# A graph layer on one core: one pipeline stage per iteration, more gathers put together from columns

## The chip, the cores and the metric

The kernel runs on one core of a Trainium2 chip. The metric is the device time of one execution in microseconds, as the median of several runs. The core has five engines that work side by side, each through its own queue in order: TensorE (PE, with weight loads shown as PEld), VectorE (DVE), ScalarE (ACT), GpSimd (POOL) and SyncE (SP), which starts DMAs.

## The reference

12500 nodes with 64 features, 200000 edges sorted by target (`dst`), with random sources (`src`):

```python
ssp(v) = softplus(v) - log(2)
gates = (ssp(edge_attr @ We1 + be1) @ We2 + be2) * (1 - sigmoid(5 * (dist - 3.5)))
h = ssp(concat(x[src], x[dst]) @ Wn1 + bn1) @ Wn2 + bn2
message_sum = zeros_like(x).at[dst].add(h * gates)
new = x + (ssp(message_sum @ Ws1 + bs1) @ Ws2 + bs2)
out = layernorm(x + new)
```

Edge layers go from 64 to 64 features, node layers from 128 to 128 and to 64. All is float32.

## The kernel before

The edges are cut into 391 groups of 512. A group is four lots (K = 4) of 128 edges, and one lot's source rows come by one indirect DMA that POOL issues (`gather`, L204): 128 rows of 64 floats into the tile `xg`. The half of the first node layer that belongs to the targets is a table in DRAM (x times the lower half of Wn1, plus bias), written in 98 chunks of 128 nodes in the first iterations (`chunk`, `keep_chunk`). Since targets are sorted, 256 edges touch a window of at most W = 42 nodes: SP loads the window of the table (`load`, L224, tile `wns`), and a one-hot matrix beside the source rows (`onehot`, L277) picks the row for each edge.

One group runs through these steps, named as in the code:

- PE: `transposes` of the four lots with their one-hot parts into PSUM `tx` (L283). ACT: `xcopy` to SBUF (L291).
- PE: layer 1 into PSUM tile `z`: bias (L296), edge half (L301), node half (L308). The tile `z` is two banks, with two buffers; 768 columns hold layer 1, then come 84 columns for scatter sums and 128 spare ones.
- ACT: `exps` (L322) and `logs` (L325) into SBUF tile `u`. DVE: `softplus` (L330), one operation on `u` and on `z`.
- PE: layer 2 into PSUM `gh` (bias L347, edge L354, node L359). DVE: `hcut` (L368) and `message` (L372).
- PE: `scatter` (L376), the messages times the one-hot matrices, into the 84 columns of a later `z`. DVE: `window` (L396), two additions into `sums` at addresses held in registers.

Some lots are not gathered. x also lies in SBUF as columns (`xh`), and for a chosen lot 128 copies of one column each, at addresses from registers (`columns`, L259, on ACT and DVE), build the source rows already transposed. `read_columns` (L242) loads those addresses from SBUF into registers, `choose` (L271) picks the right half, and an extra product with `wn1_twice` takes the place of the gather. `COLUMNS = (8, 16)` is the number of columns per iteration on DVE and on ACT, and `slots_by_columns` plans from it which lots they are: 70 of them, so 71 groups have three gathers (one of them because of the padding at the end) and 320 have four.

`busy` (L334) is a product that nobody reads, issued so that PE doesn't pause: one before the node half of layer 1 where no chunk stands there, one before layer 2. Whenever the sums of a block of 512 nodes are complete, a node block follows (25 of them): `hidden` (L415), `clamp` (L430, L431), `logs`, `ssp`, second layer (L446), `add`, and the layer norm (`square`, `variance`, `root`, `scale` L472, `store`), spread over later iterations by `BLOCK_STEPS`.

The order on every engine is written by hand (`manual_schedule`): what stands earlier in the loop body is earlier in that engine's queue, and the tile framework adds waits where data or buffers need them. Iteration i gathers group i + 3, does layer 1 for group i + 1, layer 2 and messages for group i and the scatter for group i - 2. A gather waits for its buffer, one of eight: in iteration i for the scatter of group i - 5, which PE issues three iterations earlier. The last groups and the last node block are written out by hand after the loop, and from twelve groups before the end (`CLOSE`) two scatters move one iteration closer.

Of the kernel before, what the change touches and what calls it, by code (L numbers as in the profile page):

```python
# [92 lines left out]
def chunk_of(i, NCH):  # L93

    c = i + CHUNKS
    return c if i >= 0 and c < NCH else None


def nodes_ready(g, NCH):

    return min(NCH, CHUNKS * (1 + max(0, (g - LOADS) // CHUNKS))) * P


@with_exitstack
def gnn_resnorm_kernel(ctx: ExitStack, tc: tile.TileContext, a: dict, out: bass.AP, E: int):
# [10 lines left out]
    REST = LOADS + 2  # L116
# [9 lines left out]
    loads = inner.enter_context(tc.tile_pool(name="loads", bufs=LOADS + 2, side="right"))  # L126
# [44 lines left out]
    columns_at = const.tile([P, sum(columns_of)], I32, name="columns_at")  # L171
    wn1_twice = const.tile([P, 2 * D], F32, name="wn1_twice")
# [22 lines left out]
    def gather(g, part=range(K), needs=()):  # L195

        if part[0] == 0:
            xgs[g] = loads.tile([P, K, P], F32, name="xg", bufs=AHEAD + BEHIND)
        xg = xgs[g]
        for k in part:  # L200
            if padding(g, k) or (g, k) in by_columns:
                nc.vector.memset(xg[:, k, :D], 0.0)
                continue
            behind(note(("gather", g), nc.gpsimd.indirect_dma_start(  # L204
                out=xg[:, k, :D], out_offset=None, in_=x,
                in_offset=bass.IndirectOffsetOnAxis(ap=src_i[:, g, k : k + 1], axis=0))), *needs)
            needs = ()
# [3 lines left out]
    def load(g):  # L211
        old = ("scatter", g - LOADS - 4)
# [18 lines left out]
    column_at, columns_done, whole = [[], []], [0, 0], []  # L231
# [4 lines left out]
    def read_columns(i, queue):  # L236

        if columns_left(i, queue) <= 0:
            return
        n, count = columns_done[queue], COLUMNS[queue]  # L240
        p, q = (n // count) % P, queue * columns_of[0] + n // (count * P) * count
        column_at[queue] = nc.values_load_multi_w_load_instructions(  # L242
            columns_at[p : p + 1, q : q + count], engines=[engines[queue][1]], min_val=xh_at,
            max_val=xh_at + 4 * (half_n - 1), skip_runtime_bounds_check_because="src holds rows of x")[1]
# [19 lines left out]
    def choose(pool):  # L264

        while whole:
            queue, g, k = slot = whole.pop(0)
# [6 lines left out]
    xTs, zs, us, ss, ghs, hs, msgs, scs = ({} for _ in range(8))  # L274
# [4 lines left out]

    def transposes(g, *needs):  # L280
        tx = tx_tile()[:DW].rearrange("f (k e) -> f k e", k=K)
# [7 lines left out]
    def xcopy(g):  # L289
        xT = work.tile([DW, K, P], F32, name="xT", bufs=3)  # L290
# [3 lines left out]
    def layer1_bias(g, *needs):  # L294
        zs[g] = z_tile()
# [21 lines left out]
    every, edge, node = slice(0, 3 * HE), slice(0, HE), slice(HE, 3 * HE)  # L317

    def exps(g, part=every):
        if part.start == 0:  # L320
            us[g] = work.tile([P, 3 * HE], F32, name="u")
        nc.scalar.activation(us[g][:, part], z_of(g)[:, part], AF.Exp)  # L322

    def logs(g, part=every):
        nc.scalar.activation(us[g][:, part], us[g][:, part], AF.Ln, bias=one)  # L325

    def softplus(g, part=every):
        if part.start == 0:
            ss[g] = work.tile([P, 3, 2, P], F32, name="s", bufs=3)
        nc.vector.scalar_tensor_tensor(ss[g].rearrange("p i t e -> p (i t e)")[:, part], us[g][:, part], BIG,  # L330
                                       z_of(g)[:, part], OP.min, OP.max)
# [7 lines left out]
    opened = {}  # L339

    def busy_before_layer2(g):
        opened[g + 1] = gh_tile()
        busy(opened[g + 1][:, :P])

    def layer2_bias(g):
        gh = opened.pop(g) if g in opened else gh_tile()
# [9 lines left out]
    def layer2_node(g):  # L356
        for h in range(2):
            for t in range(2):
                nc.tensor.matmul(ghs[g][:, 1, 2 * t + h, :], ss[g][:, 1 + h, t, :], wn2, start=False,  # L359
                                 stop=h == 1 and t == 1, skip_group_check=True)  # L360

# [4 lines left out]
    def hcut(g):  # L366
        hs[g] = work.tile([P, K, D], F32, name="h")
        nc.vector.tensor_mul(hs[g], ghs[g][:, 1], cut[:, g, :].to_broadcast([P, K, D]))  # L368

    def message(g):  # L370
        msgs[g] = work.tile([P, K, D], F32, name="msg", bufs=3)
# [26 lines left out]
    def node_block(first, n, pool):  # L398
# [7 lines left out]
        def tile3(name):  # L406
            return pool.tile([P, 2, 2, D], F32, name=name, bufs=3)[:p, :nq]
# [4 lines left out]
        def hidden(z):  # L412
            t["z"] = z[:, :HE]
            for q in range(nq):
                nc.tensor.matmul(t["z"], ws1[:, q].rearrange("f o d -> f (o d)"),  # L415
                                 sums[:, first + q * HE : first + (q + 1) * HE], start=q == 0, stop=q == nq - 1,
                                 skip_group_check=True)

        def fetch():
            t["y"] = tile3("y")  # L420
            nc.sync.dma_start(t["y"], x[rows, :].rearrange("(q p k) d -> p q k d", q=nq, k=2))
# [5 lines left out]

        def clamp():
            t["l"], t["zb"] = (pool.tile([P, HE], F32, name=name, bufs=2) for name in ("l_s", "zb"))
            nc.vector.tensor_scalar(t["l"], t["z"], packed["bs1"], BIG, OP.add, OP.min)  # L430
            nc.vector.tensor_scalar(t["zb"], t["z"], packed["bs1"], None, OP.add)  # L431
# [8 lines left out]
        def layer2(z):  # L440
            slots = t["l"].rearrange("f (p k) -> f k p", k=2)
            t["u"] = z[:p, :HE].rearrange("p (q k d) -> p q k d", q=2, k=2)
            nc.tensor.matmul(z[:p, :HE], ones3[:, :p], rs3.rearrange("q k d -> q (k d)"), start=True,
                             stop=False, skip_group_check=True)
            for k in range(2):
                nc.tensor.matmul(t["u"][:, :, k, :], slots[:, k, :p], ws2, start=False, stop=k == 1,  # L446
                                 skip_group_check=True)

        def add():
            nc.vector.scalar_tensor_tensor(t["y"], t["y"], 2.0, t["u"][:, :nq], OP.mult, OP.add)  # L450

        def square():
            t["y2"] = tile3("y2")
# [23 lines left out]
        return [Part(None, fetch), Part(hidden, clamp), Part(None, logs), Part(None, center), Part(None, ssp),  # L477
                Part(layer2, add), Part(None, square), Part(None, variance), Part(None, root), Part(None, scale),
                Part(None, store)]

    def node_part(part):
        if part.tensor:
            part.tensor(gh_tile())
        part.others()

    with tc.manual_schedule():
# [4 lines left out]
        xT = sums[: D + 1, : NCH * P].rearrange("d (c p) -> d c p", p=P)  # L491
# [3 lines left out]
        def load_x(first, last):  # L495
            nc.sync.dma_start(xT[:, first:last, :], a["xT"][:, first:last, :])

        dst_h = prep.tile([P, NR, HE], I32, name="dst_h")
# [5 lines left out]
        nc.sync.dma_start(src_i[:, :HEAD, :], cols[:, :HEAD, :])  # L504
        nc.scalar.dma_start(dst_h, a["dst_h"])
        load_x(0, CHUNKS)
        nc.scalar.dma_start(consts[:, :FIRST], a["consts"][:, :FIRST])
        nc.sync.dma_start(dst_i[:, :HEAD, :], targets[:, :HEAD, :])
# [5 lines left out]
        load_x(CHUNKS, 2 * CHUNKS)  # L514

        for g in range(AHEAD):
            gather(g)
# [24 lines left out]
        for c in range(CHUNKS):  # L542
            nc.tensor.matmul(ps[:, c, :], xT[:, c, :], wnb, start=True, stop=True)
# [4 lines left out]
        spread = prep.tile([P, NR, P], F32, name="spread")  # L548
        base_b = prep.tile([P, NR * P], F32, name="base_b")
# [66 lines left out]

        def highest():
# [10 lines left out]
        def far():  # L628
            ps = tx_tile()
# [13 lines left out]
        def chunk(c, z):  # L643
            if c % CHUNKS == 0:
                tbs[c // CHUNKS] = piece()
            nc.tensor.matmul(z, xT[:, c, :], wnb, start=True, stop=True, skip_group_check=True)
# [6 lines left out]
        cuts = [2 * CHUNKS, 4 * CHUNKS, 6 * CHUNKS, 9 * CHUNKS, 12 * CHUNKS, NCH]  # L653
        beside = {0: [lambda: nc.sync.dma_start(src_i[:, HEAD:, :], cols[:, HEAD:, :])],
                  1: [lambda: nc.sync.dma_start(columns_i, a["columns"]), load_wn1, lambda: load_xh(0)],
                  2: [lambda: load_xh(1), far], 3: [lambda: load_xh(2)], 4: [lambda: load_xh(3), places],
                  5: [lambda: load_x(cuts[0], cuts[1])],
                  6: [lambda: nc.sync.dma_start(dst_i[:, HEAD:, :], targets[:, HEAD:, :])],
                  7: [lambda: load_x(cuts[1], cuts[2])], 10: [lambda: load_x(cuts[2], cuts[3])],
# [292 lines left out]
```

## Time and profile before

| | |
|---|---|
| median of three runs | 2363.53 us (2359.99 to 2370.90) |
| profiled execution | 2389.88 us, span 2388.1 us, mean granted clock 0.981 |
| PE | 1970.5 us busy (83% of the span), 12897 instructions |
| PE weight loads | 1656.7 us (69%) |
| ACT | 1511.2 us (63%), 7412 instructions |
| POOL | 1417.0 us (59%), 1497 instructions, 1493 of them gathers |
| DVE | 1293.9 us (54%), 5966 instructions |

Busy times of an engine are added over its instructions; an engine that waits is not busy. All figures of the trace are of the profiled execution. A row of the timeline gives the start, the duration, the engine, the source line, the operation with its output and inputs, and in brackets the idle time before it with what ended it. A row of the groups gives the count, the total busy time and the mean in nanoseconds of one, then the idle time just before.

### The profile page before, as it was taken

The page shows a single profiled execution, that of the slowest core. Times are in us where ns is not written, and L with a number is a line of the kernel's source. Part 1 is how long each engine was busy: PE and PEld are TensorE (multiplying, and loading weights), DVE is VectorE, ACT ScalarE, POOL GpSimd, SP SyncE. Part 2 cuts the span into 40 slices and gives each one's busy share as a digit, 9 for nine tenths or more (in the row PEclk, how much of TensorE's full clock was granted, in tenths as well). Part 3 has the DMA queues.
Part 4 walks back from the last instruction along what each step waited for, and adds up shares of the span by engine and source line. Part 5 has one row for each costly group of instructions (what it writes and reads, how often), then busy time and mean ns, then how long its engine had stood idle before and what let it go on. Part 6 is the DMA issues. An engine that isn't in the chain of part 4 may idle for free.

```text
span 2388.1 us, 48209 instructions
## 1 busy us (share of the span) xinstructions
PE 1970.5 (83%) x12897; PEld 1656.7 (69%) x12897; DVE 1293.9 (54%) x5966; ACT 1511.2 (63%) x7412; POOL 1417.0 (59%) x1497
## 2 busy tenths in 40 slices
PE   6788888888888888888888888888888888888877
PEld 4666677767776776677677667766777767777765
DVE  4355555555555555555555555555555555555544
ACT  3466666666666666666666666666666666666653
POOL 5665665666666666666666666665665666666650
PEclk9799999999999999999999999999999999999988
DMA  6332232322222222222222222222222222222220
GB/s 185 85 91 68 56 75 56 77 61 71 54 57 56 53 59 54 57 56 62 53 59 55 57 58 55 59 59 54 58 58 56 59 57 60 63 57 58 59 50 14
DMA packets 159679, 148.63 MB, mean 62 GB/s; under 512 B 40564, under 2 KB 108949, under 8 KB 159274
## 3 DMA queue, kind: packets, MB, share of 16 engines
q1 hardware_dynamic: 111194, 94.97, 14.4%
q0 software_dynamic: 47776, 49.02, 10.8%
q8 instruction: 109, 1.79, 0.3%
q14 instruction: 166, 1.36, 0.2%
q10 hardware_dynamic: 434, 1.50, 0.2%
HBM read 135.70 MB, written 9.62 MB: 61 GB/s over the span
## 4 chain that ended last, share of the span: by engine, by line
PE 80%; issue 13%; ACT 3%; DVE 2%; another core or an unknown queue 1%; DMA 0%; DVEq 0%; ACTq 0%
PE z L308 18%; PE gh L359 13%; PE z L376 10%; PE tx L283 10%; PE gh L354 7%; PE z L301 6%; PE gh L334 4%; PE gh L347 3%; PE z L296 3%; PE z L334 2%; ACT xT L291 2%; PE tx L415 1%; PE tx L446 1%; PE z L311 1%
## 5 line engine op out<-in xcount | busy, mean ns | idle before, releaser
L204 POOL DMA_INDIRECT xg<-in_x,src_i x1493 | 1416.8, 949 | 919.3 <-PE tx L283 488.8
L308 PE MATMUL z<-xT,wns 106*128 106x256 f32 x1564 | 459.7, 412 | 359.9 <-issue 285.9
L291 ACT COPY xT<-tx 106x512 f32<-106x512 f32 x391 | 229.1, 586 | 779.3 <-PE tx L283 751.1
L259 ACT COPY column<-xh 128x4 uint8 x6016 | 608.7, 193 | 0.0
L308 PEld LDWEIGHTS z<-xT,wns 106*128 106x128 f32 x1564 | 267.8, 193 | 452.4 <-issue 337.7
L368 DVE TENSOR_TENSOR h<-gh,cut 128x256 f32<-128x256 f32 x391 | 165.9, 424 | 747.9 <-PE tx L283 632.2
L359 PE MATMUL gh<-consts,s 128*128 128x64 f32 x3128 | 396.0, 270 | 0.0
L359 PEld LDWEIGHTS gh<-consts,s 128*128 128x128 f32 x3128 | 385.0, 194 | 0.1
L325 ACT ACTIVATE u<-u,one 128x768 f32<-128x768 f32 x392 | 365.8, 933 | 13.4 <-ACT u L322 0.5
L330 DVE SCALAR_TENSOR_TENSOR s<-u,z 128x768 f32<-128x768 f32 x392 | 368.7, 941 | 0.4 <-issue 0.4
L322 ACT ACTIVATE u<-z 128x768 f32<-128x768 f32 x392 | 314.7, 803 | 43.4 <-PE z L308 19.0
L396 DVE TENSOR_TENSOR sums<-sums,z 64x42 f32 x778 | 152.4, 196 | 291.3 <-issue 207.4
L376 PEld LDWEIGHTS z<-xg,msg 128*128 128x128 f32 x1556 | 205.0, 192 | 140.6 <-issue 121.3
L376 PE MATMUL z<-xg,msg 128*128 128x84 f32 x1556 | 265.1, 293 | 15.3 <-DVE msg L372 15.3
L259 DVE COPY column<-xh 128x4 uint8 x2944 | 246.5, 219 | 0.4 <-issue 0.4
L354 PE MATMUL gh<-consts,s 128*128 128x128 f32 x1564 | 243.3, 279 | 1.3 <-DVE s L330 0.8
L283 PE MATMUL tx<-consts,xg 128*106 128x128 f32 x1564 | 238.1, 276 | 0.0
L301 PE MATMUL z<-eT,consts 128*128 128x256 f32 x782 | 237.3, 386 | 0.0
L354 PEld LDWEIGHTS gh<-consts,s 128*128 128x128 f32 x1564 | 210.0, 195 | 2.0 <-DVE s L330 1.1
L283 PEld LDWEIGHTS tx<-consts,xg 128*106 128x106 f32 x1564 | 182.5, 142 | 0.9 <-issue 0.9
L372 DVE TENSOR_TENSOR msg<-gh,h 128x256 f32<-128x256 f32 x391 | 165.8, 424 | 13.4
L334 PEld LDWEIGHTS gh<-consts 128*128 128x128 f32 x778 | 149.5, 195 | 20.5 <-issue 0.3
(109 smaller groups left out, 1456.2 us busy)
## 6 DMA issues: line engine op xcount, KB each, us to landing
eT<-in_eT SPq DMA_DIRECT2D x195, 256.0 KB
xg<-in_x,src_i POOLq DMA_INDIRECT x1493
wns<-table SPq DMA_DIRECT2D x782, 21.0 KB
table<-tb SPq DMA_DIRECT2D x14, 448.0 KB
side<-in_sides SPq DMA_DIRECT2D x70, 64.0 KB
y<-in_x SPq DMA_DIRECT2D x24, 128.0 KB
out<-y SPq DMA_DIRECT2D x24, 128.0 KB
xh<-in_xh SPq DMA_DIRECT2D x2, 781.5 KB
```

What stands on the lines that cost most here:

```text
L204: behind(note(("gather", g), nc.gpsimd.indirect_dma_start(out=xg[:, k, :D], out_offset=None, in_=x, in_offset=bass.IndirectOffsetOnAxis(ap ...
L259: copy(column_tiles[slot].bitcast(U8)[:, 4 * r : 4 * r + 4], xh[:, bass.ds(column_at[queue][j] - xh_at, 4)])
L283: ins = nc.tensor.transpose(tx[:, k, :], xgs[g][:, k, :DW], ident)
L301: nc.tensor.matmul(zs[g][:, 0, :HE], we1.rearrange("a h d -> a (h d)"), eTs[g], start=False, stop=True, skip_group_check=True)
L308: nc.tensor.matmul(zn, wns[:, g % REST, h, :], xTs[g][:, h], start=True, stop=not chosen, skip_group_check=True)
L322: nc.scalar.activation(us[g][:, part], z_of(g)[:, part], AF.Exp)
L325: nc.scalar.activation(us[g][:, part], us[g][:, part], AF.Ln, bias=one)
L330: nc.vector.scalar_tensor_tensor(ss[g].rearrange("p i t e -> p (i t e)")[:, part], us[g][:, part], BIG, z_of(g)[:, part], OP.min, OP.max)
L334: nc.tensor.matmul(z, we1.rearrange("a h d -> a (h d)"), ident, start=True, stop=True, skip_group_check=True)
L354: nc.tensor.matmul(v[:, 0, t], ss[g][:, 0, t, :], we2, start=False, stop=False, skip_group_check=True)
L359: nc.tensor.matmul(ghs[g][:, 1, 2 * t + h, :], ss[g][:, 1 + h, t, :], wn2, start=False, stop=h == 1 and t == 1, skip_group_check=True)
L376: ins = nc.tensor.matmul(sc, msgs[g][:, 2 * t : 2 * t + 2, :].rearrange("p h f -> p (h f)"), xgs[g][:, 2 * t : 2 * t + 2, D:DW], start=t = ...
```

## The change

Every step now has an iteration of its own (`LAGS`): in iteration i the kernel gathers group i + 3 and transposes group i, then xcopy works on group i - 1, layer 1 on i - 2, exps and logs on i - 3, softplus on i - 4, layer 2 on i - 5, hcut and message on i - 6, the scatter on i - 7 and the window addition on i - 9.

- A new copy on ACT (`keep`) moves layer 1's 768 columns, the scatter sums and a node block's product from `z` in PSUM to an SBUF tile `c`. softplus and window read that tile instead of `z`.
- A gather waits for the layer-2 products that PE issued in its iteration before (`layer2` of group i - 6) and for the transposes of group i - 2; `xg` has twelve buffers instead of eight.
- `COLUMNS = (20, 12)`: 94 lots instead of 70 are built from columns, so 95 groups have three gathers and 296 have four. DVE makes 20 copies per iteration and ACT 12. DVE's addresses are loaded in two halves, one issued behind softplus and one behind hcut and message. `choose` comes one iteration later.
- `busy` is issued only where the group that is gathered in this iteration has four gathers: once before the node half (if no chunk and no node-block product stands there), once before the transposes. The one before layer 2 is gone. 444 such products are left of 688.
- PE's order in an iteration is: layer-1 bias, scatter, layer-2 bias and layer 2, edge half, then a chunk, a node-block product or `busy`, node half, `busy`, transposes.
- A node block copies its sums first (`take`), its two layers go in products of 128 columns into the spare columns of `z`, one per iteration, and the gaps between its steps stand in the list that `node_block` returns.
- The first eight groups' source indices are loaded first, several steps of the preparation move into iterations 1 to 4, and the closing part that was written out by hand gives way to the same loop, which runs until the node blocks are done.

The core of the diff (the rest is the preparation, the node block's new parts and the removal of the closing part):

```diff
-LOADS = 5
+FIRST_ROWS = 8
+FREE = 3
+REST = 7
 SPREADS = 5
-PREPARE = 5
-BEHIND = 5
-CLOSE = 12
-
-
-BLOCK_STEPS = ((2, 3, 4, 4, 6, 7, 8, 9, 10, 14), (2, 3, 3, 4, 5, 6, 7, 8, 9, 10), (1, 2, 1, 2, 3))
-COLUMNS = (8, 16)
+LAGS = dict(xcopy=1, z=2, exps=3, softplus=4, layer2=5, message=6, sums=7, window=9)
+BUFS = AHEAD + LAGS["sums"] + 2
+GATE = AHEAD + 2
+FETCH = 3
+PACE = None
+PAUSE = 1
+
+
+COLUMNS = (20, 12)
...
-            if (g - 3 - COLUMNS_FROM + 1) * columns >= (n + 1) * P and not {g - 1, g, g + 1} & taken:
+            if columns and (g - 1 - COLUMNS_FROM) * columns >= (n + 1) * P and not {g - 1, g, g + 1} & taken:
...
-    def gather(g, part=range(K), needs=()):
-
-        if part[0] == 0:
-            xgs[g] = loads.tile([P, K, P], F32, name="xg", bufs=AHEAD + BEHIND)
-        xg = xgs[g]
-        for k in part:
+    def gather(g):
+        xgs[g] = loads.tile([P, K, P], F32, name="xg", bufs=BUFS)
+        xg, needs, n = xgs[g], [("layer2", g - AHEAD - 1 - LAGS["layer2"]), ("transposes", g - GATE)], 0
+        if PACE == "landing":
+            needs.append(("last", g - 1))
+        for k in range(K):
             if padding(g, k) or (g, k) in by_columns:
                 nc.vector.memset(xg[:, k, :D], 0.0)
                 continue
-            behind(note(("gather", g), nc.gpsimd.indirect_dma_start(
+            ins = note(("gather", g), nc.gpsimd.indirect_dma_start(
                 out=xg[:, k, :D], out_offset=None, in_=x,
-                in_offset=bass.IndirectOffsetOnAxis(ap=src_i[:, g, k : k + 1], axis=0))), *needs)
-            needs = ()
+                in_offset=bass.IndirectOffsetOnAxis(ap=src_i[:, g, k : k + 1], axis=0)))
+            behind(ins, *needs)
+            needs, n = [], n + 1
+        made["last", g] = [ins]
...
-        old = ("scatter", g - LOADS - 4)
+        old = ("transposes", g - GATE)
...
-    def read_columns(i, queue):
-
-        if columns_left(i, queue) <= 0:
+    def read_columns(i, queue, part=0, parts=1):
+
+        if not 0 <= i < NG or columns_left(i, queue) <= 0:
             return
+        if part == 0:
+            column_at[queue] = []
         n, count = columns_done[queue], COLUMNS[queue]
         p, q = (n // count) % P, queue * columns_of[0] + n // (count * P) * count
-        column_at[queue] = nc.values_load_multi_w_load_instructions(
-            columns_at[p : p + 1, q : q + count], engines=[engines[queue][1]], min_val=xh_at,
+        first, last = (count * j // parts for j in (part, part + 1))
+        column_at[queue] += nc.values_load_multi_w_load_instructions(
+            columns_at[p : p + 1, q + first : q + last], engines=[engines[queue][1]], min_val=xh_at,
...
+        ready = list(chosen_next)
+        chosen_next[:] = whole
+        del whole[:]
+        for slot in ready:
+            queue, g, k = slot
...
+    def gathered(g):
+        return sum(not padding(g, k) and (g, k) not in by_columns for k in range(K)) if 0 <= g < NG else 0
+
     def transposes(g, *needs):
-        tx = tx_tile()[:DW].rearrange("f (k e) -> f k e", k=K)
+        tx = tx_tile()
+        if gathered(g + AHEAD) == K:
+            busy(tx[:, :P])
+        tx = tx[:DW].rearrange("f (k e) -> f k e", k=K)
...
+    def keep(z, n, summed, extra):
+
+        ends = (0, 3 * HE, 3 * HE + 2 * W, 3 * HE + 2 * W + P)
+        held = [n is not None, summed is not None, bool(extra)]
+        c, at = None, 0
+        while at < 3:
+            end = at
+            while end < 3 and held[end]:
+                end += 1
+            if end > at:
+                c = work.tile([P, ends[3]], F32, name="c") if c is None else c
+                nc.scalar.copy(c[:, ends[at] : ends[end]], z.rearrange("p b e -> p (b e)")[:, ends[at] : ends[end]])
+            at = end + 1
+        if c is None:
+            return
+        if n is not None:
+            cs[n] = c[:, : 3 * HE]
+        if summed is not None:
+            scs[summed] = c[:, 3 * HE : 3 * HE + 2 * W]
+        return c[:, 3 * HE + 2 * W :]
+
+    def softplus(g):
+        ss[g] = work.tile([P, 3, 2, P], F32, name="s")
+        nc.vector.scalar_tensor_tensor(ss[g].rearrange("p i t e -> p (i t e)"), us[g], BIG, cs[g], OP.min, OP.max)
...
+        return [(0, Part(None, take)), (1, hidden(0)), (1, hidden(1)), (1, Part(None, center)),
+                (2, Part(None, logs)), (1, Part(None, ssp)), (1, layer2(0))] + [(1, layer2(q)) for q in range(1, nq)] + [
+                (3, Part(None, square)), (1, Part(None, variance)), (1, Part(None, root)), (1, Part(None, scale)),
+                (2, Part(None, store))]
...
+            i = -AHEAD
+            while i <= NG + lag["window"] or blocks:
+                zt = z_tile()
+                n = i - lag["z"]
+                if 0 <= n < NG:
+                    zs[n] = zt
+                spare = zt[:, 1, HE + 2 * W : HE + 2 * W + P]
+                at(load, i + FETCH)
+                at(gather, i + AHEAD)
+                at(layer1_bias, n, ("load", n))
+                summed = i - lag["sums"]
+                at(scatter, summed, zt[:, 1, HE : HE + 2 * W])
+                at(layer2_bias, i - lag["layer2"])
+                at(layer2, i - lag["layer2"])
+                at(layer1_edge, n)
...
+                if free and 0 <= n < NG and gathered(i + AHEAD) == K:
+                    busy_before_node(n)
+                at(layer1_node, n)
+                at(transposes, i, ("gather", i), ("onehot", i))
+
+                at(xcopy, i - lag["xcopy"])
+                at(exps, i - lag["exps"])
+                extra = keep(*kept)
+                at(logs, i - lag["exps"])
+                if chunked:
+                    keep_chunk(*chunked)
+                chunked = None if c is None else (c, spare)
+                kept = zt, n if 0 <= n < NG else None, summed if 0 <= summed < NG else None, after
+
+                at(softplus, i - lag["softplus"])
+                read_columns(i, 0, 0, 2)
+                at(hcut, i - lag["message"])
+                at(message, i - lag["message"])
+                read_columns(i, 0, 1, 2)
+                at(onehot, i + 1)
+                at(window, i - lag["window"])
+                if waiting:
+                    waiting[0](waiting[1])
+                waiting = (kept_part, extra) if kept_part else None
...
+                read_columns(i, 1)
+                for queue in (1, 0):
+                    if 0 <= i < NG:
+                        columns(i, queue, finish)
+                if 0 <= i < NG:
+                    choose(finish)
```

`PACE` is `None`, so its branches do nothing.

More of the change, by code (lines that the diff above doesn't have):

```diff
@@ L315, in z_of, with exps, logs @@
         return zs[g].rearrange("p b e -> p (b e)")[:, : 3 * HE]
[L317 to L331, printed above, removed]
+    def exps(g):
+        us[g] = work.tile([P, 3 * HE], F32, name="u")
+        nc.scalar.activation(us[g], z_of(g), AF.Exp)
+    def logs(g):
+        nc.scalar.activation(us[g], us[g], AF.Ln, bias=one)
+    def keep(z, n, summed, extra):
[20 more added lines that the diff above has]
+        nc.vector.scalar_tensor_tensor(ss[g].rearrange("p i t e -> p (i t e)"), us[g], BIG, cs[g], OP.min, OP.max)
     def busy(z):
@@ L513, in gnn_resnorm_kernel @@
                           a["Wn1"][:D, :].rearrange("f (r o) -> f r o", r=1).to_broadcast([D, 2 * REST, 2 * D]))
[L514 to L517 removed]
+        load_x(1)
         nc.vector.memset(one, 1.0)
@@ L740, in gnn_resnorm_kernel @@
-                if blocks and complete >= blocks[0][1]:
-                    steps = next(steps for steps in BLOCK_STEPS if i + steps[-1] < last - 1)
-                    for n, part in zip(steps, begun):
-                        parts.setdefault(i + n, []).append(part)
-                    rest = begun[len(steps) :]
-                    blocks.pop(0)
-                    begun = None
-            assert len(blocks) == 1 and begun and not parts
-            begun.pop(2).others()
-            transposes(last, ("load", last), ("gather", last), ("onehot", last))
@@ L752, in gnn_resnorm_kernel @@
-            xcopy(last)
-            layer1_bias(last)
-            layer2_bias(last - 1)
-            scatter(last - 2, zs[last][:, 1, HE : HE + 2 * W])
-            layer1_edge(last)
-            layer1_node(last)
-            for some in (edge, node):
-                exps(last, some)
-                logs(last, some)
-            square, variance, root, scale, store = (part.others for part in rest)
-            square()
-            window(last - 2)
-            for g in range(last - 1, last + 1):
-                if g not in window_at:
-                    window_bases(g)
@@ L865, in gnn_resnorm_kernel @@
         for block in node_blocks(N):
-            for part in node_block(*block, o):
+            for _, part in node_block(*block, o):
                 node_part(part)
```

253 lines of the change are left out of this document (103 added, 150 removed).

## The prediction

> **What bounds the kernel now.** I read the stage first, then the waits, then the timeline of POOL. One stretch of the middle, in the view by windows (busy us and instructions of PE, its weight loads, DVE, ACT and POOL, then the granted clock, DMA share and GB/s), and the group of the gathers:
>
> ```profile
> 583.00:2285.00 1702.00, 1428.22 (x9504) 1203.38 (x9502) 944.40 (x4434) 1117.29 (x5576) 1040.63 (x1097) 1.00 0.25 58
> ```
>
> ```profile
> L204 POOL DMA_INDIRECT xg<-in_x,src_i x1493 | 1416.8, 949 | 919.3 <-PE tx L283 488.8 <-issue 349.5 <-PE z L376 20.0
> ```
>
> No engine is full, and the TensorE clock is at 1.00. The 1097 gathers of the stretch are 287 groups (1493 gathers in 391 groups are 3.82 each), so a group takes 5.93 us, with 4.98 of PE, 3.89 of ACT, 3.29 of DVE and 3.63 of POOL. Each waits for another. The view of waits gives total us, times and longest us:
>
> ```profile
> ACT xT L291 <- PE tx L283: 751.1, 375, 12.0
> DVE h L368 <- PE tx L283: 632.2, 279, 2.8
> POOL xg L204 <- PE tx L283: 488.8, 342, 7.2
> ```
>
> Three engines wait in nearly every iteration for the same event of PE, the transposes. The timeline shows how late that event is:
>
> ```profile
> 1207.66 0.60 PE L283 MATMUL tx<-consts,xg 128*106 128x128 f32 x4
> ...
> 1209.56 0.42 DVE L368 TENSOR_TENSOR h<-gh,cut 128x256 f32<-128x256 f32 x1 [2.79 <-PE tx L283]
> 1209.69 0.59 ACT L291 COPY xT<-tx 106x512 f32<-106x512 f32 x1 [2.40 <-PE tx L283]
> 1209.87 0.94 POOL L204 DMA_INDIRECT xg<-in_x,src_i  x1 [1.49 <-PE tx L283]
> ```
>
> The transposes end at 1208.26; the copy that needs only them starts 1.43 us later, together with DVE and POOL. POOL's wait of 1.49 us began when its last gather ended, at 1208.38. I read this so: while a run of gathers is under way, what PE has finished becomes visible to the others only when the last gather of the run has landed. POOL then is its own clock, and its timeline fits that:
>
> ```profile
> 1598.61 0.95 POOL L204 DMA_INDIRECT xg<-in_x,src_i  x1 [1.42 <-PE tx L283]
> ...
> 1603.33 0.95 POOL L204 DMA_INDIRECT xg<-in_x,src_i  x1 [1.28 <-PE tx L283]
> 1604.58 0.94 POOL L204 DMA_INDIRECT xg<-in_x,src_i  x1 [0.30 <-issue]
> ...
> 1609.52 0.94 POOL L204 DMA_INDIRECT xg<-in_x,src_i  x1 [1.49 <-PE tx L283]
> ```
>
> A group with three gathers (the first) takes 4.72 us from start to start, one with four 6.19: a gather costs 1.25 (0.94 and an issue of 0.30) and each run one wait of about 1.4.
>
> **The change part by part.** The sum is made against the profiled execution, 2389.88 us, which lies 26.35 above the median of the runs, 2363.53; I take that off at the end.
>
> *Fewer gathers.* By the planner's condition with (20, 12) instead of (8, 16), 94 instead of 70 gathers are put together from columns, so 24 more groups have three. 24 x (6.19 - 4.72) = **-35 us**. It rests on the cadence staying POOL's.
>
> *The other engines' stage.* The rows for what comes and goes:
>
> ```profile
> L259 ACT COPY column<-xh 128x4 uint8 x6016 | 608.7, 193 | 0.0
> L259 DVE COPY column<-xh 128x4 uint8 x2944 | 246.5, 219 | 0.4 <-issue 0.4
> L330 DVE SCALAR_TENSOR_TENSOR s<-u,z 128x768 f32<-128x768 f32 x390 | 367.6, 943 | 0.4 <-issue 0.4
> L544 ACT COPY tb<-z 128x896 f32<-128x896 f32 x1 | 0.9, 906 | 7.0 <-issue 7.0
> ```
>
> ```profile
> L242 DVEq TENSOR_LOAD <-columns_at x368: 593/611/1436, 104.2 to 2275.9; - x184
> ```
>
> ```profile
> 1205.12 0.39 PE L334 MATMUL gh<-consts 128*128 128x128 f32 x2
> ```
>
> A column copy costs 608.7/6016 = 0.101 us on ACT and 246.5/2944 = 0.084 on DVE (busy time over count, since they overlap). ACT loses four and gains the copy of z, scatter sums and block product into SBUF (852 columns, by the 896-column row some 0.87): 3.89 - 0.40 + 0.87 = 4.4 us. DVE gains twelve copies, 3.29 + 1.01 = 4.3, and a second register load; each takes 0.6 and lies behind softplus (0.94) or behind hcut and message (0.42 each); if the cover fails it costs up to 0.6 apiece, so DVE is between 4.3 and 5.5. PE keeps 444 of 688 unread products, each 0.39 for its two records in the timeline: 244 x 0.39/391 = 0.24 less, so 4.7; node blocks give it the same work in smaller products. All lie under 6.19. In groups of three gathers, 4.72, PE drops both unread products and DVE is about level. Cost on the path: 0, with up to 95 x (5.5 - 4.72) = 74 us if both loads are bare. Softplus, exps and logs moved a stage later have a whole iteration to wait in; what is late next is POOL again.
>
> *The gate of the gathers.* gather(i+3) now waits for the layer-2 products that PE issued one iteration earlier, instead of the scatter that it issued three iterations earlier, so POOL can run less far ahead. Behind the wait on POOL stand only later gathers; who waits for them is a transpose three iterations on. SP's load waits for transposes(i-2) and has three iterations of lead, so it costs nothing. Where PE's signal comes before the hold begins, POOL goes straight on and two runs join. The trace has two kinds of joined eight gathers, shown by their first gather and the first after them:
>
> ```profile
> 28.70 0.94 POOL L204 DMA_INDIRECT xg<-in_x,src_i  x1 [7.22 <-PE tx L283]
> ...
> 40.59 0.94 POOL L204 DMA_INDIRECT xg<-in_x,src_i  x1 [2.19 <-remote]
> ...
> 2287.97 0.94 POOL L204 DMA_INDIRECT xg<-in_x,src_i  x1 [1.44 <-remote]
> ...
> 2301.80 0.94 POOL L204 DMA_INDIRECT xg<-in_x,src_i  x1 [4.14 <-DVE l_s L430]
> ```
>
> Two runs of four apart take 12.38 us. Joined they took 11.89 (-0.49), and 13.83 (+1.45) where the wait ended with a node block's step. Since the new order lets at most one block product into an iteration, I stay near the first, at -0.25, for one pair in four groups: 98 x -0.25 = **-24**, bounds -48 and +142.
>
> *Softplus reads two SBUF tiles.* In before its second operand is z in PSUM. What a two-SBUF operation does to a gather is in the trace:
>
> ```profile
> 1566.11 0.42 DVE L472 TENSOR_TENSOR y<-y,rstd 128x256 f32<-128x256 f32 x1
> 1566.21 1.14 POOL L204 DMA_INDIRECT xg<-in_x,src_i  x1 [0.30 <-issue]
> ```
>
> That gather lasts 1.14 instead of 0.94 and ends 0.82 after the DVE operation. The 390 softplus of 0.94 us in before cannot have done so to many gathers, whose mean is 0.949. Softplus now waits for the same layer-2 signal as the first gather. From the release in the timeline above, DVE starts 0.31 before POOL: a softplus starting there ends 0.63 into the gather, which would end 0.82 later, 0.51 late. That is the upper bound, 391 x 0.51 = +199; the lower is 0, where DVE is still at its twenty columns when the signal comes and softplus starts after the gather's read. With runs that join, POOL often gets its signal while DVE is behind. I take half of it in one group of four: 98 x 0.25 = **+24**, and keep both ends.
>
> By the Trainium skill ("SBUF — State Buffer", section "Who interferes with whom") a DVE instruction with two SBUF inputs contends with a GpSimd instruction that reads SBUF, and one with a single SBUF input does not; the two rows agree. By that rule the sum would be rival A's.
>
> *Start and end.* The copies of the first groups, and the last runs:
>
> ```profile
> L291 ACT COPY xT<-tx x9: 566/586/586, 28.5 to 91.4; 106x512 f32<-106x512 f32 x9
> ```
>
> ```profile
> 2309.48 0.95 POOL L204 DMA_INDIRECT xg<-in_x,src_i  x1 [4.07 <-DVE s L330]
> ...
> 2317.40 0.99 POOL L204 DMA_INDIRECT xg<-in_x,src_i  x1 [3.22 <-PE z L376]
> ...
> 2332.80 0.94 POOL L204 DMA_INDIRECT xg<-in_x,src_i  x1 [3.01 <-PE z L376]
> ```
>
> Eight periods from 28.5 to 91.4 take 62.9 us, 13 more than eight of 6.19. The new prologue moves the later bases and the highest targets into iterations 1 to 4 and reads eight rows of src first; I take half, **-7** (-13 to +7). At the end, from 2287.97 to 2332.80 (two runs in 13.8, one of three in 7.68, three in 23.3), 44.8 us pass for five runs of four and one of three, against 5 x 6.19 + 4.72 = 35.7: 9 too many, as the closing order sets in. It goes, but the pipeline is several stages longer when the gathers are over, by work that then runs at 4.7 an iteration: **-2** (-9 to +20).
>
> Sum: -35 - 24 + 24 - 7 - 2 = -44. 2389.88 - 44 - 26.35 = **2319.5**, say 2319 us.
>
> **The rivals.** What a measurement here can tell from no change is about 0.5%, 12 us: under 2351.7 is faster, over 2375.3 slower.
>
> *A, slower: softplus locks out the first gather.* For it: both wait for one signal, the DVE at 4.3 to 5 us is done before a 6.19 period ends, and the order of starts in the timeline (DVE 0.31 ahead). Against: it needs DVE to be idle at the release. It decides from a mean delay of 44/391 = 0.11 us a group, where it has eaten the gain. In every group, with no joins: 2319 - (-24 + 24) + 199 = 2518. In half of them, with my joins: 2319 - 24 + 100 = 2395. It lies between the two.
>
> *B, no change: the clock.* After a pause of PE the trace has
>
> ```profile
> 193.57 2.07 PE L308 MATMUL z<-xT,wns 106*128 106x256 f32 x4 [2.66 <-issue]
> ```
>
> ```profile
> 193.40:196.80 3.40, 3.23 (x11) 2.87 (x12) 0.51 (x2) 1.64 (x17) 2.60 (x3) 0.51 0.15 28
> ```
>
> a granted clock of 0.51 for 3.4 us. With 244 unread products gone and joined runs that leave PE without work, such pauses can come back. Each costs 1.7 us of PE's work, of which 6.19 - 4.7 = 1.5 is slack, unless two follow each other. One whole loss per pair in a third of the 98: +56, 2375; fewer: 2350. The Trainium skill ("TensorE: Matmul & The Clock Gate", section "HAM oscillation") describes a clock that drops again in waits within a loop. The row agrees.
>
> *C, slower: the change does not hide the loads.* If both register loads stand bare instead of behind softplus and the messages, the change does not do what it says, and DVE with 5.5 us sets the 95 groups of three gathers: 2319 + 74 = 2393. For it: a load took up to 1.436 us, longer than any cover. Against: the median is 0.611, under either cover.
>
> *D, faster still.* Every run joins in pairs and softplus always misses the read: 195 x -0.49 = -96 instead of -24 + 24: 2319 - 96 = 2223.
>
> **How the numbers follow.** My case 0.42, by its own bounds 2285 to 2350; A 0.24; B 0.13, of which half counts as the same; C 0.09; D 0.12. Faster: 0.41 + 0.12 + 0.02 (the light end of B) = 0.55. Same: 0.01 + 0.08 = 0.09. Slower: 0.24 + 0.09 + 0.03 = 0.36. The range of 8 in 10 runs from D's 2223 to 2450, into A, leaving out A's upper half and half of D.
>
> **What would show it.** Right: gathers 1469, the periods in the middle 6.1 and 4.7 with some runs joined, POOL's waits ending with PE's layer 2, gathers at a mean near 0.96 us, clock 1.00 in the middle. A shows as a mean of a gather well over 1.0 and first gathers of about 1.45; B as windows at 0.5 in the clock's row; C as POOL's waits ending with DVE and DVE idle only at its loads; D as waits of POOL in fewer than half of the groups. The forecast is wrong if the period of a group with four gathers leaves 6.0 to 6.3, for then POOL's cadence is not what I take it for.

## The result and the profile after

| | before | after |
|---|---|---|
| median | 2366.28 us | 2706.90 us |
| runs | 2359.99 to 2370.90 | 2699.48 to 2715.74 |
| profiled span, mean clock | 2388.1 us, 0.981 | 2697.6 us, 0.834 |

The change makes the kernel slower by 14.4% (ratio 1.1443, 95% interval 1.1391 to 1.1495); 2319 with 2223 to 2450 had been forecast. The page of after, busy times and the chain that ended last:

```profile
PE 2355.1 (87%) x12675; PEld 1928.4 (71%) x12675; DVE 1674.2 (62%) x10744; ACT 1646.2 (61%) x6276; POOL 1494.0 (55%) x1473
...
DVE 47%; DVEq 25%; PE 10%; issue 8%; POOL 4%; DMA 3%; another core or an unknown queue 1%; ACT 1%; ACTq 0%; POOLq 0%; SPq 0%
DVEq L255 23%; DVE column L272 17%; DVE s L368 10%; DVE msg L404 5%; DVE h L400 4%; DVE sums L428 4%; POOL xg L209 4%; DMA xg<-in_x,src_i 2%; DVE xg L293 2%; PE gh L390 2%; PE z L329 2%; PE gh L385 1%; DVE chosen L287 1%; DVEq L417 1%
```

PE no longer leads the chain, DVE does, and its largest single line is none of its operations: L255, the register load of column addresses in DVE's queue (DVEq). The same stretch of the middle as in the prediction, by windows:

```profile
583.00:2285.00 1702.00, 1500.22 (x8184) 1228.42 (x8183) 1078.66 (x7056) 1067.62 (x4154) 964.80 (x953) 0.85 0.22 51
```

953 of 1469 gathers are 254 of 391 groups: 6.71 us a group instead of 5.93, with 4.25 of DVE and 4.21 of ACT. DVE works 4.25 us and has a loop of 6.71. One turn of that loop, on DVE's timeline:

```profile
1417.61 1.51 DVE L272 COPY column<-xh 128x4 uint8 x20
1419.03 0.58 DVE L287 SCALAR_TENSOR_TENSOR chosen<-side,column 64x128 f32<-64x128 int32 x2
1419.63 0.96 DVE L368 SCALAR_TENSOR_TENSOR s<-u,c 128x768 f32<-128x768 f32 x1
1420.51 0.42 DVE L400 TENSOR_TENSOR h<-gh,cut 128x256 f32<-128x256 f32 x1
1420.96 0.42 DVE L404 TENSOR_TENSOR msg<-gh,h 128x256 f32<-128x256 f32 x1
1423.54 0.33 DVE L293 TENSOR_TENSOR xg<-consts,rel 128x168 f32<-128x168 f32 x1 [2.15 <-DMA xg<-in_x,src_i]
```

Between message and onehot DVE is idle for 2.15 us. The releaser named is a gather, but between the two instructions stands the second register load. The chain of the same turn, piece by piece (start, duration, what), gives that time to it:

```profile
1420.96 0.42 DVE msg L404
1421.39 1.90 DVEq L255
...
1423.54 0.10 DVE xg L293
```

The loads by line (minimum, median and maximum in ns), DVE's and ACT's:

```profile
L255 DVEq TENSOR_LOAD <-columns_at x756: 1061/2166/3391, 65.5 to 2632.7; - x189
L255 ACTq TENSOR_LOAD <-columns_at x374: 767/798/1095, 68.9 to 2603.9; - x187
```

In the trace the two loads of an iteration alternate all the way through: 1.09 us for the first half and 2.36 for the second in the median, and no second one is under 2.29. DVE loads ten addresses in 2.36 us where ACT loads twelve in 0.80.

### The profile page after: what moved, and what is told of

The parts are those of the page before. It is cut to its first block, busy times and chain, and to the rows that moved or that the text cites. A ratio compares the mean times of both kernels' runs of the same rounds, so it can differ in the third digit from the quotient of the medians.

```text
span 2697.6 us, 51423 instructions
## 1 busy us (share of the span) xinstructions
PE 2355.1 (87%) x12675; PEld 1928.4 (71%) x12675; DVE 1674.2 (62%) x10744; ACT 1646.2 (61%) x6276; POOL 1494.0 (55%) x1473
## 4 chain that ended last, share of the span: by engine, by line
DVE 47%; DVEq 25%; PE 10%; issue 8%; POOL 4%; DMA 3%; another core or an unknown queue 1%; ACT 1%; ACTq 0%; POOLq 0%; SPq 0%
DVEq L255 23%; DVE column L272 17%; DVE s L368 10%; DVE msg L404 5%; DVE h L400 4%; DVE sums L428 4%; POOL xg L209 4%; DMA xg<-in_x,src_i 2%; DVE xg L293 2%; PE gh L390 2%; PE z L329 2%; PE gh L385 1%; DVE chosen L287 1%; DVEq L417 1%
## 5 line engine op out<-in xcount | busy, mean ns | idle before, releaser
L209 POOL DMA_INDIRECT xg<-in_x,src_i x1469 | 1493.8, 1017 | 1148.6 <-PE gh L390 506.2
L356 ACT COPY c<-z 128x852 f32<-128x852 f32 (+4 forms) x402 | 352.7, 877 | 532.5 <-DVE sums L428 272.4
L293 DVE TENSOR_TENSOR xg<-consts,rel 128x168 f32<-128x168 f32 x391 | 130.5, 334 | 809.4 <-issue 418.5
L272 DVE COPY column<-xh 128x4 uint8 x7552 | 594.4, 187 | 7.6 <-issue 2.0
L390 PE MATMUL gh<-consts,s 128*128 128x64 f32 x3128 | 478.1, 306 | 1.6 <-issue 1.6
L272 ACT COPY column<-xh 128x4 uint8 x4480 | 462.8, 198 | 22.3 <-issue 22.1
L390 PEld LDWEIGHTS gh<-consts,s 128*128 128x128 f32 x3128 | 467.8, 229 | 1.9 <-issue 1.9
L368 DVE SCALAR_TENSOR_TENSOR s<-u,c 128x768 f32<-128x768 f32 x391 | 366.4, 937 | 21.5 <-ACT u L343 8.5
L322 PE MATMUL z<-eT,consts 128*128 128x256 f32 x782 | 324.9, 505 | 0.0
L385 PEld LDWEIGHTS gh<-consts,s 128*128 128x128 f32 x1564 | 234.1, 215 | 102.9 <-issue 102.6
L428 DVE TENSOR_TENSOR sums<-sums,c 64x42 f32 x782 | 153.1, 196 | 68.7 <-issue 63.5
```

The source lines that it names most:

```text
L209: ins = note(("gather", g), nc.gpsimd.indirect_dma_start(out=xg[:, k, :D], out_offset=None, in_=x, in_offset=bass.IndirectOffsetOnAxis(ap= ...
L272: copy(column_tiles[slot].bitcast(U8)[:, 4 * r : 4 * r + 4], xh[:, bass.ds(column_at[queue][j] - xh_at, 4)])
L322: nc.tensor.matmul(zs[g][:, 0, :HE], we1.rearrange("a h d -> a (h d)"), eTs[g], start=False, stop=True, skip_group_check=True)
L356: nc.scalar.copy(c[:, ends[at] : ends[end]], z.rearrange("p b e -> p (b e)")[:, ends[at] : ends[end]])
L385: nc.tensor.matmul(v[:, 0, t], ss[g][:, 0, t, :], we2, start=False, stop=False, skip_group_check=True)
L390: ins = nc.tensor.matmul(ghs[g][:, 1, 2 * t + h, :], ss[g][:, 1 + h, t, :], wn2, start=False, stop=h == 1 and t == 1, skip_group_check=True)
```

## The experiments

**The theories.** L: the second load is long because its ten words start 40 bytes into their row, which is no multiple of 16, and are then read one by one; it sets DVE's loop, and the low clock follows from PE's pauses. P: the place behind the messages makes it long. A: softplus with two SBUF inputs delays the gathers. B: the low clock itself costs the time. J came later: runs of gathers that join keep PE's results back. C, F and G are explained in the expectations that use them.

The kernel before takes 1992 to 1994 us on four of the chips that the experiments ran on and 2396 on the fifth, so each time below is to be read against the kernel before on its own chip.

**First set** (before 1993.61 us).

```diff
e1  -        first, last = (count * j // parts for j in (part, part + 1))
    +        first, last = ((0, 12, 20)[j] if parts == 2 else count * j for j in (part, part + 1))
e2  -                read_columns(i, 0, 0, 2)
    +                read_columns(i, 0)
    -                read_columns(i, 0, 1, 2)
e3  -        if gathered(g + AHEAD) == K:          (and the same condition before the node half)
e4  (before) +  columns_at two words further in: q = 2 + queue * (columns_of[0] + 2) + ...
```

e1: 

> The 20 addresses of an iteration are loaded as 12 and 8 instead of 10 and 10, in the same two places; nothing else differs. Theory L (the second load is long because it starts 40 bytes into its row, which is not a multiple of 16, and so is read word by word): the first load takes 0.8 us as ACT's loads of twelve do, the second 0.6 as the loads of eight before, instead of 1.07 and 2.30; DVE's idle time between message and onehot falls from 2.0 to about 0.4 us, the loop from 6.9 to about 5.9 us per group, and the time to 2300 to 2420 us. Theory P (the place behind the messages makes the second load long, whatever it reads): the second load stays at 1.9 us or more and the time within 3% of 2707. Theory A (softplus and the gathers set the loop): the loads shorten, the time stays over 2600.

Measured 2036.8, ratio 1.0257 (1.0201 to 1.0313). The loads take 0.87 and 0.61 us in the median, in the places they had. P is refuted.

e2: 

> One load of all 20 addresses behind softplus, none behind the messages. Theory L: the load starts 16-byte aligned and takes 0.2 + 5 x 0.21 = 1.25 us, of which softplus hides most; the idle time before onehot goes, hcut waits up to 0.4 us; 2300 to 2440 us. Theory P: the load behind softplus stays near 1.1 to 1.3 us as the first half does, and the time falls in the same way, so this run does not tell L from P. Theory A: over 2600.

Measured 2000.4, ratio 1.0047 (1.0024 to 1.0070); the load of twenty takes 1.39 us.

e3: 

> The two unread products stand in every iteration, also where the group gathers three. Theory L (DVE sets the loop, the low TensorE clock follows from PE's pauses): within 1.5% of 2707, clock up by 0.05 or more. Theory B (the lower clock sets the time): over 4% less than 2707, under 2600 us.

Measured 2651.6, ratio 1.3304 (1.3281 to 1.3326), clock 0.847. The unchanged kernel takes 2654.7 on such a chip (k1). The clock rose by less than the 0.05 expected (0.825 to 0.847), so this run alone is a weak test of B. What refutes B are h1 (below), e1 and e2, which leave PE's work as it is and change the loads alone: the time falls and the clock rises with it, to 0.945, 0.986 and 0.986.

e4: 

> The kernel before, with the address tile shifted by two words, so that DVE's loads of eight and ACT's of sixteen start 8 bytes past a multiple of 16. Theory L: DVE's loads take 0.2 + 8 x 0.21 = 1.9 us instead of 0.61 and ACT's 0.2 + 16 x 0.21 = 3.6 instead of 1.04; DVE idles 2.7 us per iteration there, so its own share costs nothing, ACT's 2.6 us more may cost up to 1 us per group: 2370 to 2750 us. Theory P: both loads as before, 0.61 and 1.04, and the time within 0.5% of 2366.

That text is wrong in one thing: ACT's addresses came to lie four words further, still at a multiple of 16 bytes. The loads by line, of e4:

```profile
L242 ACTq TENSOR_LOAD <-columns_at x376: 1002/1037/1267, 66.1 to 1935.0; - x188
L242 DVEq TENSOR_LOAD <-columns_at x368: 1840/1901/2912, 74.4 to 1897.5; - x184
```

Eight words at an offset of 8 bytes take 1.90 us instead of 0.61, in another kernel and at another place in the queue, as L has it. The time is 1996.9, ratio 1.0022 (1.0013 to 1.0032): in before DVE has the time to spare, and the long load alone costs little.

**Second set** (before 2396.33 us): f1 the change as it is; f2 e2 without `busy`; f3 e2 with `COLUMNS = (8, 16)`; f4 before without `busy`.

f1: 

> The changed kernel as it is, for comparison beside the others. Theory L: as on record, some 14% above the kernel before where that takes 2366 us; where the kernel before takes 1994 us the loop is DVE's all the same, 6.6 to 6.9 us per group, 2600 to 2710 us, 30 to 36% above it.

Measured 2722.1, ratio 1.1351 (1.1322 to 1.1379).

f2: 

> One load of 20 as in the second experiment, and no unread products at all (444 fewer of 0.39 us, 173 us of PE). Theory G (without the long load PE or POOL sets the loop; POOL with 1469 gathers of 0.95 to 1.02 and an issue of 0.30 needs 1840 to 1940 us): 1900 to 1985 us where the kernel before takes 1994. Theory C (the unread products hold the clock up; without them PE pauses, runs at half rate and is late): 2050 us or more, mean clock under 0.95.

Measured 2470.1, ratio 1.0283 (1.0262 to 1.0303), clock 0.827.

f3: 

> One load as in the second experiment, and 8 and 16 columns instead of 20 and 12, so 70 lots from columns instead of 94. Theory G (PE is the bound where the kernel before takes 1994 us, so fewer gathers buy nothing): within 1% of 2000 us, and at 2320 to 2420 where the kernel before takes 2366. Theory F (the gathers set the time): 24 x 1.25 = 30 us or more slower than the second experiment's 2000.

Measured 2495.3, ratio 1.0414 (1.0388 to 1.0441), clock 0.871; 75 us over the range given for this chip. On this kind of chip something besides the long load costs about 3 to 4%.

f4: 

> The kernel before without its 688 unread products (268 us of PE). Theory G: where the kernel before takes 1994 us with PE busy 98% of the time, the next bound is POOL with 1493 gathers of 1.25, 1870 us and what lies around them: 1920 to 1985 us. Theory C: PE pauses in each iteration, the clock falls under 0.95, and the time is 2050 us or more.

Measured 2439.1, ratio 1.0209 (1.0148 to 1.0269), clock 0.894 (0.973 to 0.981 with them, on the same chip). The unread products earned something in before, as C has it, though the interval leaves open whether it is 2%; the numbers given for the other chip weren't tested.

**Third set** (before 1993.82 us).

```diff
g2  -PACE = None
    +PACE = "landing"
g3       at(hcut, ...), at(message, ...)
    +    at(softplus, i - lag["softplus"])      (moved from ahead of hcut)
    +    read_columns(i, 0)
```

g1: 

> The second experiment's kernel once more, beside the next three. Where the kernel before takes about 1994 us: 2000, as there. Where it takes 2366 to 2396 us: 2440 to 2500, since f3 with 24 more gathers took 2495 and f2 without unread products 2470.

Measured 2004.1, ratio 1.0061 (1.0041 to 1.0082).

g2: 

> One load of 20, and PACE set to landing: a group's first gather also waits until the last gather of the group before has landed, so no two runs join. Where the kernel before takes 2366 to 2396 us: theory J (joined runs keep PE's results back for longer and the pauses halve the clock) 2300 to 2400, clock 0.95 or more; theory A (softplus delays the gathers) 2440 or more, gathers at a mean over 1.02. Where the kernel before takes 1994 us the landing of 1.1 us comes into each group: 2150 to 2350.

Measured 2760.3, ratio 1.3844 (1.3804 to 1.3883): 1.93 us more a group than g1, far over the range; gathers and their landings now stand in the chain with 13% each. This chip can't tell J, and the wait for the landing is no remedy here.

g3: 

> One load of 20, with softplus and the load behind hcut and message instead of ahead of them, so that softplus starts 0.84 us later and lies past the read of the first gather. Theory A: the mean of a gather falls from 1.02 to 0.98 or less, and the time falls by 60 us or more against g1 where the kernel before takes 2366 to 2396. Theory J: within 1.5% of g1.

Measured 2015.1, ratio 1.0101 (1.0075 to 1.0126). Gathers have a mean of 1.03 us, not under 0.98: moving softplus did not take their delay away, and it gains nothing here.

g4: 

> g2 without unread products. Theory J with the clock as its second half: PE has 4.2 us of work in a period of 6, pauses, and the clock falls again: 60 us or more above g2 and a clock under 0.93. If the clock is not what costs time: within 1.5% of g2.

Measured 2776.4, ratio 1.3946 (1.3851 to 1.4041), clock 0.779 after 0.823 in g2: within 1.5% of g2 in spite of the clock.

**Fourth set** (before 1993.04 us). h1 keeps both loads of ten where they are and changes the layout alone; h2, h3 and h4 are e2, g3 and f2 again.

```diff
-            columns_at[p : p + 1, q + first : q + last], ...
+            columns_at[p : p + 1, q + first + 2 * part : q + last + 2 * part], ...
         (each block of 20 addresses lies in 24 words: ten, two empty, ten, two empty)
```

h1: 

> The changed kernel with two loads of ten in the same places; only the layout differs: each block of twenty addresses takes 24 words, so that the second half starts 48 bytes in instead of 40. Theory L (word by word from an offset that is not a multiple of 16): the second load takes 1.07 us as the first does, instead of 2.30, and DVE's idle time before onehot falls from 2.0 to 0.7 to 0.9; 2100 to 2200 us where the kernel before takes 1994, 2480 to 2560 where it takes 2366 to 2396. Theory P: 2.3 us and no change.

h2: 

> One load of twenty. Where the kernel before takes 1994: 2000 again. Where it takes 2366 to 2396: by theory L the long load is most of the 14%, and 2440 to 2500 us is left, 3 to 4% above before.

h3: 

> Softplus behind hcut and message. Where the kernel before takes 1994: 2015 again. Where it takes 2366 to 2396: theory A (softplus delays the first gather of each run) at least 60 us under h2; theory J (what is left comes from runs that join and from the clock) within 1.5% of h2.

h4: 

> One load and no unread products. Where the kernel before takes 2366 to 2396: 2470 as in f2. Where it takes 1994, PE being busy 98% of the time: theory G 1900 to 1970 us, since 173 us of PE go and POOL needs 1469 times 1.25 to 1.32; theory C (the clock falls) 2050 or more.

Measured: h1 2180.9, ratio 1.0939 (1.0910 to 1.0968); h2 2001.3, 1.0044 (1.0029 to 1.0060); h3 2014.3, 1.0104 (1.0077 to 1.0131); h4 2002.9, 1.0058 (1.0038 to 1.0077). In h1 the two empty words bring the second load to the length of the first:

```profile
L255 DVEq TENSOR_LOAD <-columns_at x756: 1058/1091/2429, 57.9 to 2121.5; - x189
```

h4 misses G's 1970: PE's busy time falls only from 1957.3 (e2) to 1924.9, not by the 173 us of the unread products. The lower clock, 0.965 after 0.986, makes up some 40 us of the difference (an estimate from the ratio of the two); the rest is not explained.

**Fifth set** (before 1991.80 us), side by side.

k1: 

> The changed kernel as it is. Theory L: DVE's loop with the load of 2.30 us sets it on either chip: 2600 to 2730 us, so 30 to 36% above before where that takes 1994, 13 to 15% where it takes 2366 to 2396.

k2: 

> One load of twenty. 2000 where the kernel before takes 1994; 2440 to 2500 where it takes 2366 to 2396, 3 to 4% above before.

Measured: k1 2654.7, ratio 1.3316 (1.3279 to 1.3354); k2 2002.3, ratio 1.0046 (1.0030 to 1.0063). Loading the twenty addresses at once takes off 652 of the change's 663 us. The group of the onehot (busy, mean ns, and the idle time just before it) follows the time, in k1, h1, e1 and k2, in this order:

```profile
L293 DVE TENSOR_TENSOR xg<-consts,rel 128x168 f32<-128x168 f32 x391 | 130.6, 334 | 811.3 <-DMA xg<-in_x,src_i 439.4 <-issue 371.9
```

```profile
L293 DVE TENSOR_TENSOR xg<-consts,rel 128x168 f32<-128x168 f32 x391 | 130.4, 334 | 330.9 <-issue 246.8 <-DMA xg<-in_x,src_i 84.1
```

```profile
L293 DVE TENSOR_TENSOR xg<-consts,rel 128x168 f32<-128x168 f32 x391 | 133.2, 341 | 147.5 <-issue 114.5 <-DMA xg<-in_x,src_i 33.0
```

```profile
L293 DVE TENSOR_TENSOR xg<-consts,rel 128x168 f32<-128x168 f32 x391 | 127.4, 326 | 0.2
```

The four ran on three chips, where the kernel before takes 1991.8 (k1, k2), 1993.0 (h1) and 1993.6 (e1). From k1 to h1 480 us of this idle time go and 474 of the run; from h1 to e1 183 and 144; the last 147 are worth only 35, because PE then is the bound. The page of k2:

```profile
PE 1968.7 (98%) x12675; PEld 1630.8 (81%) x12675; DVE 1686.6 (84%) x10744; ACT 1618.4 (80%) x6276; POOL 1498.6 (74%) x1473
...
PE 83%; DVE 6%; DMA 3%; POOL 2%; ACT 2%; issue 2%; DVEq 1%; ACTq 0%; POOLq 0%
```

No version here beats the kernel before.

## Why the prediction was wrong

**The step that failed** is the price of a register load in the other engines' stage: "each takes 0.6", "up to 0.6 apiece", DVE "between 4.3 and 5.5", and from it at most 74 us in the groups of three gathers. I took the median of 0.611 from loads of eight words. Measured are 1.09 and 2.36 us, and the second stands bare for about 2 us in every group, not in 95 of them: 811 us of idle time in k1. DVE's busy time was right (4.25 for 4.3), but with these 2 us its loop is longer than POOL's, so DVE set the time. The row of before had no load from an offset that is no multiple of 16 bytes; its bound should have been its longest load, 1.436 us, or more: two such loads bare make 4.3 + 2.9 = 7.2 us, over the 6.19 of POOL.

The Trainium skill ("Runtime: NRT & Kernel Launch", section "Instruction fetch mechanics") puts a register load at some 200 ns per register even in bulk, for the loads that the runtime inserts. The loads here are the kernel's own and read SBUF: the measured 0.24 us a word of the second one comes near that figure, the 0.07 of ACT's twelve words does not. By it ten addresses would have been 2 us, an estimate.

**Rival C** had the right mechanism, DVE behind bare loads, and was given 0.09 and 74 us. It cost 652 us beside k2. On the chip with 2396 us, f1 lies 227 us above f3 and 252 above f2, each of which has one edit more beside the single load. The sign named for C did not show: POOL's longest waits in after end with PE's layer 2 (506 us in all), which reads what DVE's softplus writes.

**Fewer gathers**: 1469 as counted, but the 35 us rested on POOL's cadence, and POOL waited for DVE and PE.

**Rival A**: the delay exists and has the size worked out. DVE's and POOL's rows of after:

```profile
1406.94 0.95 DVE L368 SCALAR_TENSOR_TENSOR s<-u,c 128x768 f32<-128x768 f32 x1
1407.09 1.62 POOL L209 DMA_INDIRECT xg<-in_x,src_i  x1 [0.31 <-issue]
```

The gather ends at 1408.71, 0.82 after softplus, as the prediction's row had it. The Trainium skill ("SBUF — State Buffer", section "Who interferes with whom") names such a pair. The mean gather is 1.017 us. The delay did not make the loss: k1 has a mean of 1.010 and takes 2655 us, k2 has 1.020 and takes 2002. What the delay costs, g3 and h3 can't say, since moving softplus left the mean at 1.03.

**Rival B**: the clock did fall to 0.834, but as a result: h1, which moves addresses alone, brings it from 0.825 (k1) to 0.945, and e3, which gave PE its unread products back, stayed at 2652 us.

**Start, end and joins** can't be judged one by one with DVE as the bound.

**What stays open.** On the kind of chip where before takes 2366 to 2396 us, one load alone was not run, and f2 and f3 leave 74 and 99 us above before that the long load doesn't explain. By f4 the missing unread products are worth some 43 us of f2's 74, and by the prediction the 24 gathers 35 of f3's 99, so that one load alone would still leave an estimated 31 to 64 us above before, and no gain of 44. Longer runs of joined gathers, the clock of 0.83 to 0.87 and delayed gathers are all there in f2 and f3; none was separated.

The trace of f3 sizes two of them. Its 1493 gathers are as many as those of before in the prediction's row and take 1561.4 us instead of 1416.8. That is 145 us more, as rival A has it, and a run of eight takes 12.4 us from start to start in the median, no less than two runs of four, so the joins gain nothing there. Of the 187 copies of `xT` for which ACT stood idle when the transposes ended, 48 start more than 1 us later, up to 12.3. In the prediction's trace the longest such delay is 4.9, in k1 and e2 it is 0.09.

## What to carry to other kernels

Splitting a load to hide it changes where its parts start, so price each part with the size and the offset that it will have, not with the median of the old one. A move behind other work is free only if the work is longer than the moved piece as it will be. When an engine with time to spare receives almost a third more work, work out its loop with everything in its queue, the instructions that count as no busy time too.

## What the runs showed of the hardware

- Register loads from SBUF, medians: from a multiple of 16 bytes, DVE took 0.61 us for 8 words, 0.87 for 12 and 1.39 for 20, some 0.26 for every four more, and 1.09 for ten; ACT took 0.80 for 12 and 1.04 for 16. From 8 bytes past such a multiple, DVE took 1.90 for 8 and 2.36 for 10, 0.23 for every word more. That words are then read one by one is a reading of these times.
- The same kernel takes 1992 to 1994 us on four chips and 2366 to 2396 in the prediction's runs and on a fifth. In the prediction's trace a copy started 1.43 us after the transposes that it waited for had ended; in e4, the kernel before on a chip of the other kind, it is 0.04:

```profile
1208.75 0.60 PE L283 MATMUL tx<-consts,xg 128*106 128x128 f32 x4
...
1209.39 0.59 ACT L291 COPY xT<-tx 106x512 f32<-106x512 f32 x1 [1.89 <-PE tx L283]
```

Over the whole traces, where ACT stood idle when the transposes ended, that delay is 1.24 us in the median in the prediction's trace (368 copies) and never over 0.04 in e4 (371 copies). So PE's results coming late, on which the forecast's cadence rested, goes with the kind of chip: the same kernel shows it on the one and not on the other. What makes the two kinds differ, no run shows.
